# Weighing the values on 64 by 64 array tiles, and taking reciprocals on 16 columns spread by DMA

## The chip, the cores and the metric

The kernel runs on one core of one Trainium2 chip, with TensorE (PE) for matrix products, VectorE (DVE) and ScalarE (ACT) for elementwise work, GpSimd (POOL), and SyncE (SP), which here issues most DMAs. The time is the device time of one execution in microseconds. The kernel before took 3954.87 us, the median of three runs (3951.79 to 3955.97).

## The reference

The input is x, 16 images of 256 channels by 32 x 32 = 1024 positions, in float32. Two layers follow each other. In the first, positions attend to each other with 4 heads of 64 channels; in the second there is a group norm, attention with 8 heads of 32 channels, another group norm and a two-layer perceptron of width 1024. Cut to what matters:

```python
# layer 0
qkv = (xs @ w_proj + b_proj).reshape(B, S, 4, 3 * 64)
attn = softmax(einsum('bihd,bjhd->bijh', q, k) * 64 ** -0.5, axis=2)
res = einsum('bijh,bjhd->bihd', attn, v).reshape(B, S, 256)
x = res @ w_out + b_out + xs
# layer 1
x = x + attention(group_norm(x, 32 groups), 8 heads of 32) @ proj_w.T + proj_b
h = gelu(mlp_w1 @ group_norm(x) + mlp_b1)
x = x + mlp_w2 @ h + mlp_b2
```

## The kernel before

Everything is float32, and one image after another is worked on with its channels on the 128 partitions, in CC = 2 chunks. The 1024 positions are NT = 2 blocks of TB = 512 queries and SB = 8 blocks of 128 keys. Both attentions are written by one function, `attention`; "a" in a name is the first layer, "b" the second.

**The attention.** An item is a pair (t, c) of a query block and a channel chunk, so there are 4 items an image. A unit is an item and a key block, so there are 32 units. For each unit `scores` (L267) makes transposed scores, keys on the partitions, with the array in tiles of 64 x 64 (a; 2 heads a unit) or 32 x 64 (b; 4 heads a unit), and ScalarE takes their exponential e (L279). No maximum is subtracted. `weigh` (L288) then multiplies by the values, with all 128 keys as rows and the head's channels as columns: tiles of 128 x 64 in a, 128 x 32 in b, added up over 8 key blocks in one PSUM bank. VectorE adds the exponentials of the 8 key blocks (es, L305). For the softmax's denominators, `normalise` (L317) multiplies es by a matrix of ones, which puts the sum of each query on all the channels of its head (den); ScalarE copies den to d (L326) and takes exp(-d/DEN_MIN) for a check of range (L329); VectorE takes the reciprocal of 128 x 512 values (L332) and multiplies the weighted values res by it (L333). `project` is the output projection (o in a, j in b, L234), with the sum onto x and the statistics of the group norm on VectorE (L364, L368).

**The order.** Python code writes out the program's order by hand. Attention goes in steps: 3 units of a, or 1 of b; a step writes the scores of its units and then the weighings of the step before, so in a the order is 3 scores, 3 weighings, 3 scores. After each step a `Later` list ticks: `later.after(k, f)` calls f at the k-th tick from then. The denominators of an item come 2 ticks after its last weighing, the projection of a query block 3 ticks after its last denominators. So the projection o(0) comes at step 11 of the 12 of an image, and o(1) after 4 of the 8 hidden pieces that follow. Between the steps of b stand pieces of other work: the perceptron's second product of the image before (m<-g,w), and the first layer's q, k and v of the next image (qk_a, v_a). Between a and b stand the perceptron's first products of the image before (`hidden`, 8 pieces of 8 instructions each, m<-gn_h,w, L536), and q, k, v of the second layer (qk_b, v_b), which need the group norm of a's result (gm_g, gv_g for its means, gn_g for its output). When the program is built, a scheduler still moves instructions of an engine ahead of others where it expects these to wait, so the order in the trace is near that of the code, not the same.

**Projections in strips.** `product` (L234) writes a product in column strips as wide as the list `cols` says: 64 within a, 32 within b, 128 elsewhere.

**PSUM.** Eight banks: three `wide` tiles of two banks, taken in any free slot, for scores, projections and products; and two tiles of one bank (`bank`) for the accumulators, den, and the group norm's small products.

A float32 product is two instructions in the profile, so the 4096 instructions of s_a are 16 x 32 x 4 products.

## Time and profile before

| what | us |
|---|---|
| median of three runs | 3954.87 |
| profiled execution, its own time | 3953.01 |
| span of the profile | 3950.6 |
| TensorE busy | 3923.9 (99%) |
| VectorE busy | 2461.4 (62%) |
| of this RECIPROCAL, d_a and d_b | 214.5 and 214.2 |
| ScalarE busy | 2147.3 (54%) |
| den_a on TensorE | 66.6 |
| SP's DMA queue, share of 16 engines | 2.4% |

A group's line gives the line of code, the engine, the operation, output<-inputs by the program's names, the array tile as rows*columns for a matrix product, the shapes, the count, then busy time and the mean in ns of one, and after the second bar the idle time ahead of it and what ended it. L234 is a helper, so names tell its uses apart. In a timeline a line is a start and a length in us, and the number of equal instructions in a row that it merges; the ends of matrix products are modelled and overlap with the next, so the time that a row of them costs is read from start to start. Tiles that lie beside each other on the array run at once: four of 64 x 64, two of 128 x 64, four of 128 x 32.

### The profile page before, as it was taken

Reading aid. Unit: us, or ns where it says so; the run is one execution under the profiler, and the core shown is the slowest. Engines: PE = TensorE matmul, PEld = TensorE weight load, DVE = VectorE, ACT = ScalarE, POOL = GpSimd, SP = SyncE. Lnnn points to the kernel's source line nnn. Section 1 sums busy time; section 2 is a strip of 40 time slices with the busy share of each in tenths; the row PEclk is TensorE's granted clock in tenths of the full one; section 3 lists DMA queues with packets and bytes.
Section 4 is the critical chain, followed back from the end, with each engine's and each line's share of the span. In section 5 each row is a group of like instructions: output and inputs, shape, how many; then the busy total and the mean of one; then the engine's idle time right before and its main releaser. Section 6 shows DMA issues by size and latency. Waiting matters only on the chain.

```text
span 3950.6 us, 77671 instructions
## 1 busy us (share of the span) xinstructions
PE 3923.9 (99%) x34685; PEld 1407.5 (36%) x34685; DVE 2461.4 (62%) x2539; ACT 2147.3 (54%) x2815; POOL 35.3 (1%) x58
## 2 busy tenths in 40 slices
PE   9999999999999999999999999999999999999998
PEld 3324333343333423334233342333424333343335
DVE  4684756847567475674756747567474665747672
ACT  4654645546455464554645546465564655646461
POOL 1000000000000000000000000000000000000000
PEclk9999999999999999999999999999999999999999
DMA  2000000000000000000000000000000000000000
GB/s 75 1 1 7 17 1 23 1 9 15 1 23 1 9 15 1 23 1 12 12 1 23 1 23 1 1 23 1 23 1 4 20 1 23 1 4 10 1 4 20
DMA packets 18501, 42.80 MB, mean 11 GB/s; under 512 B 3728, under 2 KB 5264, under 8 KB 18160
## 3 DMA queue, kind: packets, MB, share of 16 engines
q1 hardware_dynamic: 13824, 33.56, 2.4%
q8 instruction: 273, 4.47, 0.5%
q10 hardware_dynamic: 3712, 3.80, 0.3%
q0 software_dynamic: 624, 0.41, 0.1%
q14 instruction: 68, 0.56, 0.0%
HBM read 20.99 MB, written 16.78 MB: 10 GB/s over the span
## 4 chain that ended last, share of the span: by engine, by line
PE 98%; issue 1%; DVE 1%; DMA 0%; ACT 0%; POOL 0%; POOLq 0%; DVEq 0%
PE s_b L267 14%; PE acc_b L288 12%; PE s_a L267 12%; PE acc_a L288 12%; PE m L536 12%; PE m L234 11%; PE qk_b L234 6%; PE qk_a L234 5%; PE o L234 3%; PE v_a L234 3%; PE v_b L234 3%; PE j L234 3%; PE den_b L317 1%; PE den_a L317 1%; DVE es_b L305 0%
## 5 line engine op out<-in xcount | busy, mean ns | idle before, releaser
L279 ACT ACTIVATE e_b<-s_b 128x1024 f32<-128x1024 f32 x1024 | 994.2, 1025 | 615.7 <-PE s_b L267 608.7
L305 DVE TENSOR_TENSOR es_b<-es_b,e_b 128x1024 f32<-128x1024 f32 x768 | 895.0, 1221 | 296.6 <-ACT e_b L279 296.6
L267 PE MATMUL s_b<-q,k 32*64 32x512 f32 x8192 | 598.3, 613 | 5.0 <-DVE x L364 3.2
L279 ACT ACTIVATE e_a<-s_a 128x1024 f32<-128x1024 f32 x512 | 487.3, 1026 | 180.1 <-PE s_a L267 180.1
L288 PE MATMUL acc_b<-e_b,v 128*32 128x512 f32 x4096 | 546.0, 604 | 0.0
L305 DVE TENSOR_TENSOR es_a<-es_a,e_a 128x1024 f32<-128x1024 f32 x384 | 466.4, 1215 | 32.2 <-ACT e_a L279 5.5
L267 PE MATMUL s_a<-q,k 64*64 64x512 f32 x4096 | 479.8, 598 | 0.0
L288 PE MATMUL acc_a<-e_a,v 128*64 128x512 f32 x2048 | 477.4, 600 | 0.0
L536 PE MATMUL m<-gn_h,w 128*128 128x512 f32 x1024 | 474.8, 605 | 2.0 <-DVE gn_h L414 2.0
L234 PE MATMUL m<-g,w 128*32 128x256 f32 (+1 forms) x7616 | 464.7, 379 | 0.0
L234 PEld LDWEIGHTS m<-g,w 128*32 128x32 f32 (+1 forms) x7616 | 276.1, 112 | 219.1 <-issue 57.8
L544 ACT ACTIVATE g<-m,m1b 128x512 f32<-128x512 f32 x256 | 170.3, 686 | 317.8 <-PE m L536 317.4
L305 DVE TENSOR_TENSOR es_b<-e_b,e_b 128x1024 f32<-128x1024 f32 x128 | 151.1, 1222 | 234.1 <-ACT e_b L279 234.1
L536 PEld LDWEIGHTS m<-gn_h,w 128*128 128x128 f32 x1024 | 186.1, 190 | 256.4 <-issue 190.7
L267 PEld LDWEIGHTS s_b<-q,k 32*64 32x64 f32 x8192 | 144.8, 129 | 361.9 <-issue 178.8
L332 DVE RECIPROCAL d_a<-d_a 128x512 f32<-128x512 f32 x64 | 214.5, 3352 | 64.4 <-ACT d_a L326 64.4
L234 PE MATMUL qk_a<-x,wp 128*32 128x512 f32 (+1 forms) x1856 | 245.2, 594 | 8.8 <-DMA wp<-in_L_conv_w_proj_dram 6.7
L288 PEld LDWEIGHTS acc_a<-e_a,v 128*64 128x64 f32 x2048 | 132.7, 136 | 331.1 <-issue 331.1
L267 PEld LDWEIGHTS s_a<-q,k 64*64 64x64 f32 x4096 | 139.1, 132 | 304.1 <-issue 264.1
L234 PE MATMUL qk_b<-gn_g,wq 128*32 128x512 f32 (+1 forms) x1280 | 236.9, 593 | 0.0
L288 PEld LDWEIGHTS acc_b<-e_b,v 128*32 128x32 f32 x4096 | 82.2, 108 | 406.7 <-issue 402.5
L458 DVE TENSOR_TENSOR v<-v_b,eones 128x512 f32<-128x512 f32 x64 | 44.3, 692 | 276.2 <-PE v_b L234 276.2
(107 smaller groups left out, 2408.8 us busy)
## 6 DMA issues: line engine op xcount, KB each, us to landing
x<-in_x_dram SPq DMA_DIRECT2D x32, 512.0 KB, 4.5
out_dram<-x SPq DMA_DIRECT2D x64, 256.0 KB, 2.0
w<-in_L_conv_mlp_w_dram ACTq DMA_DIRECT2D x2, 1024.0 KB, 14.9
wq<-in_L_conv_qkv_w_dram ACTq DMA_DIRECT2D x1, 768.0 KB, 11.8
wp<-in_L_conv_w_proj_dram ACTq DMA_DIRECT2D x3, 128.0 KB, 9.7
wp<-in_L_conv_w_proj_dram POOLq DMA_DIRECT2D x3, 128.0 KB, 6.9
wo<-in_L_conv_w_out_dram ACTq DMA_DIRECT2D x1, 256.0 KB, 9.3
wpj<-in_L_conv_proj_w_dram ACTq DMA_DIRECT2D x1, 256.0 KB, 13.5
```

The costliest lines, as they stand in the source:

```text
L234: nc.tensor.matmul(o[sl], w[:, sl], r, **flags)
L267: nc.tensor.matmul(tiles[g // 2][h : h + HALF, g % 2, :], kT[g * D : (g + 1) * D, c, kb * P + h : kb * P + h + HALF], qT[g * D : (g + 1) * ...
L279: nc.scalar.activation(e, s, AF.Exp, scale=scale)
L288: nc.tensor.matmul(accs[i][g * D : (g + 1) * D, :], v_of(c * G + g, kb), es[g // 2][:, g % 2, :], start=(kb == 0), stop=(kb == SB - 1),)
L305: nc.vector.tensor_add(d, held[i][n] if kb == 1 else d, e)
L317: nc.tensor.matmul(den[g * D : (g + 1) * D, :], ones_of(c * G + g), sums[i][g // 2][:, g % 2, :], start=True, stop=True,)
L332: nc.vector.reciprocal(d, d)
L458: nc.vector.tensor_mul(d, ps, v_scale.unsqueeze(1).to_broadcast([P, 2, C // D, D]))
L536: nc.tensor.matmul(ps[:, n, :], k["w1"][:, cc, hc * P : (hc + 1) * P], hn[0][:, cc, t * TB : (t + 1) * TB], start=(cc == 0), stop=(cc == C ...
L544: nc.scalar.activation(g, ps[:, n, :], AF.Gelu, bias=k["m1b"][:, hc : hc + 1])
```

## The change

The function `attention` becomes two.

- In `attention_a` the weighing goes on 64 x 64 tiles as well: the 128 keys of a block are two halves, each with its own accumulator, and the two are added when the item ends (a ScalarE copy and a VectorE addition). An item with an even number has its two accumulators in the `bank` tiles; one with an odd number in wide slot 2, which is kept out of the round meanwhile. A step is now one unit, and a unit's weighing follows its scores by two steps (34 steps an image).
- The denominators of both items of a query block of a are made together, in one bank, each sum on 32 columns in place of 64, so half of the columns pass through the array.
- `denominators` no longer takes the reciprocal of all 128 x 512 values. One row of each 32 is spread by a DMA to 128 x 16 values, VectorE takes their reciprocals, a DMA writes them to DRAM, and 2 (a) or 4 (b) DMAs read them back repeated for the channels. All are issued on SP. The exponential for the range check (`low`) reads d and comes some steps later.
- The wide PSUM tiles have three fixed slots that go round in order.
- o(0) comes at step 25 of 34, in strips of 32 columns; the last j of b comes at step 18 of the next image's a. The means of the second group norm are made on 64 x 64 tiles when they come within a. o(1) is written after 7 of the 8 hidden pieces.
- The result of b is kept in one buffer for each query block, and the second norm's output takes the buffer of q in b.

```diff
-        tc.tile_pool(name="ps_s", bufs=3, space=bass.MemoryType.PSUM)
+        tc.tile_pool(name="ps_s", bufs=1, space=bass.MemoryType.PSUM)
...
+    def wide(name, n=None):
+        while n is None:
+            if turn[0] not in kept:
+                n = turn[0]
+            turn[0] = (turn[0] + 1) % 3
+        return ps_s.tile([P, 2, TB], F32, tag=f"s{n}", name=name)
...
+    def denominators(key, d, n, waits, then, copy):
+        w = 4 * TB // P
...
+        copy(at)
+        nc.sync.dma_start(spread, d[::32].rearrange("p (a b) -> p a b", b=w))
+        def invert():
+            nc.vector.reciprocal(spread, spread)
+            nc.sync.dma_start(row.rearrange("r (a b) -> (r a) b", b=w), spread)
+            num = P * n // (4 * TB)
+            for r in range(P // num):
+                nc.sync.dma_start(
+                    full[r * num : (r + 1) * num], row[r].partition_broadcast(num)
+                )
+            later.after(waits[1], lambda: then(full))
+        def low():
+            nc.scalar.activation(
+                d, d, AF.Exp, scale=-1.0 / DEN_MIN, accum_out=lsum[:, at : at + 1]
+            )
+        later.after(waits[0], invert)
+        later.after(waits[2], low)
...
+        def weigh(i, kb, e):
+            t, c = items[i]
+            if kb == 0:
+                if i % 2:
+                    kept.add(2)
+                    acc = wide(f"acc_{key}_{i}", 2)
+                    accs[i] = [acc[:, h, :] for h in range(2)]
+                else:
+                    accs[i] = [bank(f"acc_{key}_{i}_{h}") for h in range(2)]
+            for h in range(2):
+                for g in range(2):
+                    nc.tensor.matmul(
+                        accs[i][h][g * D : (g + 1) * D, :],
+                        v[h * HALF : (h + 1) * HALF, kb, c * 2 + g],
+                        e[h * HALF : (h + 1) * HALF, g, :],
+                        start=(kb == 0),
+                        stop=(kb == SB - 1),
+                    )
...
+            if kb == SB - 1:
+                r = res[:, c, t * TB : (t + 1) * TB]
+                one, two = accs.pop(i)
+                nc.scalar.copy(r, one)
+                nc.vector.tensor_add(r, r, two)
+                kept.discard(2)
+                if c == CC - 1:
+                    later.after(1, lambda: normalise(t))
+        def normalise(t):
+            half = TB // 2
+            den = wide(f"den_{key}_{t}")[:, 0, :]
+            for c in range(CC):
+                for g in range(2):
+                    for h in range(2):
+                        j = (2 * g + h) * 32
+                        nc.tensor.matmul(
+                            den[j : j + 32, c * half : (c + 1) * half],
+                            k["ones"][:, :32],
+                            sums[t * CC + c][:, g, h * half : (h + 1) * half],
+                            start=True,
+                            stop=True,
+                        )
...
+            denominators(
+                f"{key}_{t}", d, CC * TB,
+                (2, 4, 6) if t < NT - 1 else (1, 1, 26),
...
+            nc.vector.tensor_mul(halves[0], *halves)
+            later.after(1 if t < NT - 1 else 5, lambda: project(t, res))
+        cols[0] = 32
...
+            pending.append(scores(*u))
+            if n >= lag:
+                weigh(*pending.pop(0))
...
# attention_b
-            nc.scalar.activation(
-                den, den, AF.Exp, scale=-1.0 / DEN_MIN, accum_out=lsum[:, at : at + 1]
-            )
-            nc.vector.reciprocal(d, d)
-            nc.vector.tensor_mul(r, r, d)
-            if c == CC - 1:
-                later.after(3, lambda: project(t, res[0]))
+            denominators(
+                f"{key}_{i}", d, TB,
+                ((3, 5, 7) if b + 1 < B else (1, 1, 5)) if last else (1, 3, 4),
...
+            nc.vector.tensor_mul(r, r, full)
+            if c == CC - 1:
+                wait = (10 if b + 1 < B else 1) if last else 1
+                later.after(wait, lambda: project(t, res[t]))
...
# group_norm
+            for n, sl in enumerate(halves):
+                nc.tensor.matmul(
+                    ps[sl, n, :CC], k["gavg"][sl, sl], src[sl], start=True, stop=True
+                )
...
-                    f"h{b}", xs[b], st, k["g2w"], k["g2b"], "gn", hn, 2
+                    f"h{b}", xs[b], st, k["g2w"], k["g2b"], "q1", hn,
+                    4 if b + 1 < B else 2,
```

## The prediction

> **What bounds the kernel.** I read the page's busy totals, the chain that ended last, the costliest groups, and then the timeline of TensorE through one image.

> ```profile
> PE 3923.9 (99%) x34685; PEld 1407.5 (36%) x34685; DVE 2461.4 (62%) x2539; ACT 2147.3 (54%) x2815; POOL 35.3 (1%) x58
> ...
> PE 98%; issue 1%; DVE 1%; DMA 0%; ACT 0%; POOL 0%; POOLq 0%; DVEq 0%
> ...
> L267 PE MATMUL s_a<-q,k 64*64 64x512 f32 x4096 | 479.8, 598 | 0.0
> L288 PE MATMUL acc_a<-e_a,v 128*64 128x512 f32 x2048 | 477.4, 600 | 0.0
> L332 DVE RECIPROCAL d_a<-d_a 128x512 f32<-128x512 f32 x64 | 214.5, 3352 | 64.4 <-ACT d_a L326 64.4
> ```

> TensorE carries 98% of the chain and hardly idles. So VectorE's 428 us of reciprocals (214.5, and 214.2 for d_b) lie beside it; the question is what TensorE's own order costs. Its timeline:

> ```profile
> 2909.52 1.06 PE L288 MATMUL acc_b<-e_b,v 128*32 128x512 f32 x8
> 2910.40 1.91 PE L234 MATMUL v_a<-wp,x 128*32 128x256 f32 x32
> 2912.13 1.04 PE L288 MATMUL acc_b<-e_b,v 128*32 128x512 f32 x8
> 2913.10 2.81 PE L267 MATMUL s_a<-q,k 64*64 64x512 f32 x24
> ...
> 2936.65 2.81 PE L267 MATMUL s_a<-q,k 64*64 64x512 f32 x24
> 2939.39 2.79 PE L288 MATMUL acc_a<-e_a,v 128*64 128x512 f32 x12
> 2942.01 1.03 PE L317 MATMUL den_a<-es_a,ones 128*64 128x512 f32 x4
> 2942.97 2.81 PE L267 MATMUL s_a<-q,k 64*64 64x512 f32 x24
> ```

> Columns: start, length, and the tile's shape before the operands. From start to start, 24 score instructions of 64x64, four abreast, are 6 passes of 512 columns and take 2.74 us; j's 8 passes at 2896-2900 took 3.43, so a pass is 0.429 and 6 are 2.58. The remaining 0.16 stands where the shape changes: acc_b takes 0.88 ahead of v_a of its own shape, 0.97 ahead of s_a. **One change of shape is 0.16 us.** Also important is the end of an image's hidden stage:

> ```profile
> 2999.68 1.02 PE L234 MATMUL o<-res_a,wo 128*128 128x512 f32 x2
> ...
> 3003.62 0.17 DVE L379 COPY mean_c_g<-mv_g 128x2 f32<-128x2 f32 x1
> ...
> 3005.02 0.28 PE L234 MATMUL gm_g<-mean_c_g,gavg 128*128 128x2 f32 x2
> ...
> 3008.23 1.92 DVE L414 TENSOR_SCALAR gn_g<-x,ga_g,gc_g 128x512 f32<-128x512 f32 x4
> ...
> 3013.58 1.02 PE L234 MATMUL qk_b<-gn_g,wq 128*128 128x512 f32 x2
> ```

> o ends at 3000.54. The first two gn tiles, which qk_b needs, are there at about 3009.25: a chain of 8.7 us, wholly under m matmuls.

> [...]

> **The change, part by part**, for one image.

> *Weighing on 64x64.* From 2912.13 to 2984.80 the first attention with its insertions takes 72.67, less 1.71 for four m's in it: 70.96. By counts: 128 passes of attention, and 2 acc_b, 2 den_b, 8 j, 8 o, 8 den_a are 156 x 0.429 = 66.9; 25 changes of shape x 0.16 = 4.0. The sum fits. After: 128 x 64 weighings become twice as many 64 x 64 ones, four abreast, the same passes. Changes of shape: into 64x64, out and back for j with den(0), out and back for o(0), to den(1), to m: 7. So 18 x 0.16 = **2.9 us less**. gm_h and gv_h now fit the shape.

> *Denominators on 32 columns.* den_a falls from 8 passes to 4: 4 x 0.429 = **1.7 us less**. With 0.2 kept back for new seams inside 64x64 (den after acc shows under 0.05), 4.4 x 16 = **70 us**.

> *Reciprocals.* 3352 ns for 512 columns is 6.5 ns each; 16 columns are about 0.17 us. VectorE loses 428 us and gains 96 x 0.17 = 16, 64 additions of a PSUM half at 0.75 (as the 128x512 x line) = 48, and nothing else of size. Worth nothing while TensorE is full. In the last image it isn't: s_b waits 0.85 and 1.82 us there for x's evacuation behind VectorE's queue, and j and gm wait. I take **5 us less**, between 0 and 8.

> *DMAs, all on SP.* Each of 96 denominators issues a spread, a row write and 2 or 4 broadcasts. None of this form is in the trace. Its 256 KB stores land in 2.0 us, its 512 KB loads in 4.5; [...] I take 2.5, so three legs are 7.5 us. Behind a waiting broadcast stand output stores and the next x load, needed an image later: no cost. On VectorE the reciprocal comes one step (3.8 us with a fill) after den in the second attention: den 0.86, copy 0.85 and a leg are 4.2, so it stands 0.4 us, at 4.5 a leg 2.4; behind it stand es additions, and for those the exps, through 8 e buffers. Before, the reciprocal itself held the queue 3.35. Cost 0 to 45 us in all; I take 4.

> *Fixed PSUM slots.* An odd item of the first attention keeps slot 2. Slots go round by a counter that all wide tiles of the program move on; counting it through 16 images, in 11 of 32 odd items (both of images 0 and 1, the second of 3, 5, ... 15) the scores just written lie in slot 2, and the first weighing waits for their exp: 1.03 + 0.2 latency. Elsewhere slot 2 was left a step of 1.72 us earlier. 11 x 1.23 = 14 us, or 0 if the next scores are drawn ahead; I take 8.

> *Last normalisation.* o(1) is written after hidden piece 7 of 8, before after piece 4; gm follows piece 8, and gv and gn stand ahead of qk_b with nothing written between. From gm's start to two gn tiles the trace has 3009.25 - 3005.02 = 4.2 us. Uncovered, 15 x 4.2 = 63 us. But the order on TensorE isn't the written one: o started 8 m's early here, and a last transposition of the program runs at 3884.6, 192 m's ahead of its place. So I expect o to go earlier, or m2 matmuls, which are ready, to fill the hole: 0 to 79 us, taken as 8.

> *Moved, at no cost.* o(0) goes from step 11 of 12 to step 25 of 34, and j from step 4 to step 18, where den(0) shares its excursion; both cost their 8 passes wherever they stand. Their evacuations and statistics (2 x 0.75 + 2 x 0.68 us on VectorE) come ahead of gm_h four steps, 6.9 us, later. In those VectorE has 2.9 + 4 additions of 1.22 + 0.17, about 8 us: hidden only because it also works through j and den (4.3 us); without that cover gm_h would hold TensorE some 1 us an image, 15 us. Each low exp (0.6 us, and 0.2 for its sum) moves some steps on; ScalarE has 1.03 us of exps in each step of 1.72. The output of b's second half in a buffer of its own frees ScalarE's copy from j (74 us of idle time, on an engine busy 54%): nothing. GpSimd keeps its 32 powers; none of its queue is passed.

> Sum: the profiled execution took 3953.0, with span 3950.6. 3953.0 - 70 - 5 + 4 + 8 + 8 = 3898. The median of the runs is 1.9 above the profiled one: **3900 us**.

> **The rivals.**
> (1) Normalisation partly bare, 3 us an image: 37 more, about 3937. For it: as written only piece 8 covers it. Against: the reordering.
> (2) Slower: it is quite bare, as if gm came after o as late as now (8.7 us less piece 8, 3.4): 5.3 x 15 = 79 in place of 8, 3971. The place is one, TensorE ahead of the first qk_b; from 4.2 us an image the gain is gone, from 4.7 the kernel is slower. For it: that now 1.2 us pass between mean_c (3003.79) and gm's place in the order. Against it: m2's input is complete by then.
> (3) The change doesn't do what it says: scores and weighings in one shape still pay the seam. Then 2.9 x 16 = 46 us of the 70 fall away: 3946, at the edge of no change. Against it: acc_b to v_a.
> (4) VectorE standing for late DMAs takes over from the reciprocals in the second attention: 0.8 us of TensorE for each of 64 items, some 50 more: 3950. For it: two exps of 1.03 fill ScalarE to TensorE's own pace there; against it, the idle time of VectorE (es_b waits 531 us for exps).

> **How the numbers follow.** Chances: forecast 0.52, (1) 0.22, (2) 0.12, (3) 0.06, (4) 0.08. A measurement can tell 0.2%, 8 us. Faster: forecast, (1), and a part of (3): 0.79. Same: the rest of (3), most of (4): 0.08. Slower: (2) and a little: 0.13. The forecast's own range, with bounds of the small terms, is 3878 to 3920; the range reaches over (1), (3), (4) to 3962 and leaves out (2) and the best ends.

> **What would show it.** acc_a as 64x64, x4096; some 290 fewer changes of shape; s_a and acc_a alternating at 0.86 us each; den_a at 33 us; RECIPROCAL near 0.17 us x96. Wrong would be: TensorE idle ahead of qk_b by DVE gn_g, above 1 us an image; acc_a above 0.9 us a group; es_b additions waiting behind a reciprocal.

## The result, and the profile after

The kernel after takes 4040.03 us (median, 4038.31 to 4044.91) against 3954.64 us before (here the median of four runs): a ratio of 1.0219, 95% interval 1.0201 to 1.0237. The forecast was 3900 us, faster than before. The profiled execution has a span of 4038.9 us.

The page of the kernel after: busy totals, the shares of the chain that ended last, and one of the groups (busy, mean in ns, after the second bar the idle time ahead).

```profile
PE 3928.3 (97%) x37485; PEld 1461.4 (36%) x37485; DVE 2120.1 (52%) x2569; ACT 2143.3 (53%) x2687; POOL 35.3 (1%) x58
...
PE 93%; DVE 3%; ACT 2%; DMA 1%; issue 1%; POOL 0%; SPq 0%; POOLq 0%; DVEq 0%; ACTq 0%
...
L244 PE MATMUL qk_b<-gn_g,wq 128*32 128x512 f32 (+1 forms) x1280 | 261.6, 617 | 35.2 <-DVE gn_g L576 35.2
```

TensorE's share of the chain fell from 98% to 93%: it now waits. The idle time ahead of qk_b, 35.2 us, had no counterpart before. VectorE's busy time fell by 341 us, and the time did not follow.

First the part that went as forecast. The timeline of TensorE in the first attention of the kernel after (start, length):

```profile
3255.09 1.04 PE L324 MATMUL acc_a<-e_a,v 64*64 64x512 f32 x8
3255.95 1.04 PE L302 MATMUL s_a<-q,k 64*64 64x512 f32 x8
3256.81 1.04 PE L324 MATMUL acc_a<-e_a,v 64*64 64x512 f32 x8
3257.78 3.64 PE L244 MATMUL j<-res_b,wpj 128*32 128x512 f32 x32
3261.24 1.05 PE L354 MATMUL den_a<-es_a,ones 128*32 128x256 f32 x16
```

From start to start, scores and weighings follow each other at 0.86 us for two passes (8 instructions, four at once): 0.43 a pass, and nothing where they alternate. j and den share one excursion. Counted over the trace, TensorE has 64 passes of 512 columns fewer and changes its tiling 1162 times in place of 1428.

Now the end of the hidden stage, on all engines (SPq is the issue of a DMA). It is the stretch that the prediction showed of before, one chain from the spread of den(1) to qk_b:

```profile
3048.05 0.59 SPq L262 DMA_DIRECT2D sp_a<-d_a  x1
...
3049.93 0.25 DVE L265 RECIPROCAL sp_a<-sp_a 128x16 f32<-128x16 f32 x1 [4.21 <-DMA sp_a<-d_a]
3050.22 0.34 SPq L266 DMA_DIRECT2D row_a<-sp_a  x1
...
3051.73 1.10 SPq L269 DMA_DIRECT2D rd_a<-row_a  x2
...
3056.34 1.23 DVE L377 TENSOR_TENSOR res_a<-res_a,rd_a 128x1024 f32<-128x1024 f32 x1 [6.16 <-DMA rd_a<-row_a]
...
3067.15 1.12 PE L244 MATMUL o<-res_a,wo 128*128 128x512 f32 x2
...
3078.60 0.28 PE L244 MATMUL gm_g<-mean_c_g,gavg 128*128 128x2 f32 x2
...
3079.72 0.38 PE L244 MATMUL gv_g<-tv_g,gavg 128*128 128x2 f32 x2 [0.84 <-DVE tv_g L556]
...
3081.76 1.92 DVE L576 TENSOR_SCALAR gn_g<-x,ga_g,gc_g 128x512 f32<-128x512 f32 x4
...
3082.45 9.80 PE L244 MATMUL qk_b<-gn_g,wq 128*128 128x512 f32 x16 [2.35 <-DVE gn_g L576]
```

The multiplication by rd_a is done at 3057.57, yet o starts at 3067.15: not a late DMA but o's place in TensorE's order holds it. After o stand only 16 m instructions, and all of them come ahead of gm_g. So gv_g and qk_b wait bare (0.84 and 2.35 us), and the last of the m's has itself waited 0.78 us for ScalarE. And qk_b then takes 9.64 us from start to start (v_b starts at 3092.09) where 16 such instructions are 16 x 0.429 = 6.87. The windows of the kernel after show why (columns: the window, its length, busy time and instructions of PE, PEld, DVE, ACT and POOL, the granted clock, the DMA's share, GB/s):

```profile
3067.00:3082.00 15.00, 11.48 (x29) 5.07 (x28) 4.55 (x16) 4.00 (x7) 0.69 (x1) 0.97 0.00 0
3082.00:3092.00 10.00, 9.55 (x16) 4.18 (x17) 1.67 (x4) 1.75 (x3) 0.00 (x0) 0.71 0.00 0
```

Here TensorE stood 3.5 of the 15 us before, and the clock falls to 0.71 over the next ten. This is image 12 (counted from 0), one of the worst. The same three waits come in 15 images, but qk_b then takes 6.94 us in two of them, 8.64 in nine and 9.5 to 9.7 in four: the granted clock is at 0.50 for 3.41 us in the nine and for 6.83 in the four, and stays at 1.00 in the two. For comparison, the place in the kernel before, and then image 2 of the kernel after, where the clock stayed full in spite of the waits:

```profile
3014.00:3024.00 10.00, 10.00 (x28) 5.00 (x27) 0.00 (x0) 4.35 (x7) 0.00 (x0) 1.00 0.00 0
...
580.42:590.42 10.00, 9.55 (x29) 5.45 (x30) 2.35 (x5) 3.62 (x5) 0.00 (x0) 1.00 0.00 0
```

A second place is in the first attention, in images with an odd number. The timeline of all engines of the kernel after:

```profile
3271.87 1.23 DVE L377 TENSOR_TENSOR res_a<-res_a,rd_a 128x1024 f32<-128x1024 f32 x1 [2.68 <-DMA rd_a<-row_a]
...
3274.15 0.32 DVE L550 COPY mean_h<-gm_h 64x2 f32<-64x2 f32 x2
...
3275.11 0.22 PE L533 MATMUL gv_h<-tv_h,gavg 64*64 64x2 f32 x2 [2.25 <-DVE tv_h L556]
...
3276.45 2.11 PE L324 MATMUL acc_a<-e_a,v 64*64 64x512 f32 x8
```

VectorE stands 2.68 us for rd_a. Behind it in its queue stand gm_h's small copies, whose product ended at 3269.4; gv_h waits for them on TensorE, and the weighing after it takes 2.05 us from start to start in place of 0.86: the half clock again (granted 0.50 from 3276.45 to 3278.56; by the clock's record in five of the eight odd images).

To see where the time is, the starts of the instructions give each image three stretches: a, from the first s_a to the end of its last acc_a; h+q, from there to the first s_b (hidden pieces, o(1), norm, q, k, v); and b, from there to the next s_a, with the tail in the last image. Sums over 16 images in us:

| kernel | a | h+q | b |
|---|---|---|---|
| before | 1096.6 | 752.1 | 2063.2 |
| after | 1073.3 | 851.8 | 2076.9 |

One den_b (0.99 us an image) moved from a to b; without that, b is the same. h+q lost 99.7 us: 6.6 us an image in 15 images. In a 68.77 us became 65.2 in even images and 67.8 to 69.8 in odd ones, where 63.2 was to be expected (68.77 - 2.9 - 1.7 - 0.99).

### The profile page after: what moved, and what is told of

The parts are those of the page before. It is cut to its first block, busy times and chain, and to the rows that moved or that the text cites. A ratio compares the mean times of both kernels' runs of the same rounds, so it can differ in the third digit from the quotient of the medians.

```text
span 4038.9 us, 84302 instructions
## 1 busy us (share of the span) xinstructions
PE 3928.3 (97%) x37485; PEld 1461.4 (36%) x37485; DVE 2120.1 (52%) x2569; ACT 2143.3 (53%) x2687; POOL 35.3 (1%) x58
## 4 chain that ended last, share of the span: by engine, by line
PE 93%; DVE 3%; ACT 2%; DMA 1%; issue 1%; POOL 0%; SPq 0%; POOLq 0%; DVEq 0%; ACTq 0%
PE s_b L411 13%; PE acc_b L432 12%; PE m L244 11%; PE m L692 11%; PE acc_a L324 10%; PE s_a L302 10%; PE qk_b L244 6%; PE qk_a L244 6%; PE o L244 3%; PE v_a L244 3%; PE v_b L244 3%; PE j L244 3%; PE den_b L464 2%; DVE es_a L336 1%; ACT g L700 1%
## 5 line engine op out<-in xcount | busy, mean ns | idle before, releaser
L310 ACT ACTIVATE e_a<-s_a 128x1024 f32<-128x1024 f32 x512 | 520.3, 1023 | 404.6 <-PE s_a L302 394.1
L302 PE MATMUL s_a<-q,k 64*64 64x512 f32 x4096 | 591.1, 596 | 0.2 <-DVE res_a L341 0.2
L324 PE MATMUL acc_a<-e_a,v 64*64 64x512 f32 x4096 | 588.0, 595 | 3.2 <-ACT e_a L310 3.2
L244 PEld LDWEIGHTS m<-g,w 128*32 128x32 f32 (+1 forms) x7616 | 277.9, 112 | 217.7 <-issue 65.2
L244 PE MATMUL qk_b<-gn_g,wq 128*32 128x512 f32 (+1 forms) x1280 | 261.6, 617 | 35.2 <-DVE gn_g L576 35.2
L324 PEld LDWEIGHTS acc_a<-e_a,v 64*64 64x64 f32 x4096 | 183.1, 134 | 292.2 <-issue 226.2
L302 PEld LDWEIGHTS s_a<-q,k 64*64 64x64 f32 x4096 | 172.5, 133 | 275.5 <-issue 211.5
L514 DVE SCALAR_TENSOR_TENSOR x<-o,bvo,x 128x512 f32<-128x512 f32 x64 | 45.1, 747 | 285.5 <-PE o L244 284.6
L244 PEld LDWEIGHTS qk_b<-gn_g,wq 128*32 128x32 f32 (+1 forms) x1280 | 88.5, 133 | 186.3 <-issue 161.4
```

The costliest lines, as they stand in the source:

```text
L244: nc.tensor.matmul(o[sl], w[:, sl], r, **flags)
L302: nc.tensor.matmul(s[h : h + HALF, g, :], kT[g * D : (g + 1) * D, c, kb * P + h : kb * P + h + HALF], qT[g * D : (g + 1) * D, c, t * TB : ...
L310: nc.scalar.activation(e, s, AF.Exp, scale=float(D) ** -0.5)
L324: nc.tensor.matmul(accs[i][h][g * D : (g + 1) * D, :], v[h * HALF : (h + 1) * HALF, kb, c * 2 + g], e[h * HALF : (h + 1) * HALF, g, :], st ...
```

## The experiments

Theories, by the letters of the expectations: **N**, the norm's chain is bare and the clock falls after it; **D**, the DMAs are late and TensorE waits for them; **S**, the fixed wide slots; **V**, VectorE's queue stands for rd_a and holds gm_h's copies. T, W and R are named where they come. Each run changes the kernel after, unless another is named. In brief, with ratios to the kernel before:

| run | time, us | ratio | a | h+q |
|---|---|---|---|---|
| e17_before_o_late (of before) | 4052.82 | 1.0251 [1.0235, 1.0267] | 1096.6 | 850.1 |
| e1_o_early | 3979.69 | 1.0070 [1.0053, 1.0087] | 1073.9 | 787.1 |
| e2_keep_busy | 4024.74 | 1.0179 [1.0162, 1.0196] | 1077.3 | 830.5 |
| e13_o_mid | 3951.29 | 0.9999 [0.9991, 1.0008] | 1071.9 | 763.1 |
| e3_scale_later | 4045.58 | 1.0231 [1.0214, 1.0248] | 1074.9 | 855.7 |
| e4_both | 4009.66 | 1.0144 [1.0127, 1.0161] | 1082.5 | 806.1 |
| e5_low_early | 4045.90 | 1.0237 [1.0220, 1.0254] | 1076.1 | 850.1 |
| e6_gmh_early | 4046.46 | 1.0231 [1.0214, 1.0248] | 1077.1 | 850.6 |
| e7_three | 3984.28 | 1.0076 [1.0059, 1.0093] | 1071.0 | 792.2 |
| e8_three_slot | 3986.09 | 1.0088 [1.0071, 1.0105] | 1059.9 | 805.8 |
| e10_den_bank | 4037.66 | 1.0212 [1.0195, 1.0229] | 1123.1 | 794.2 |
| e11_gmh_late | 4007.11 | 1.0139 [1.0122, 1.0156] | 1065.6 | 818.2 |
| e12_weigh128 | 4071.60 | 1.0302 [1.0285, 1.0319] | 1157.4 | 793.1 |
| e14_gmh_late_alone | 4010.18 | 1.0145 [1.0130, 1.0161] | 1048.1 | 844.3 |
| e15_mid_and_late | 3925.08 | 0.9928 [0.9915, 0.9942] | 1048.4 | 761.2 |
| e16_gm_banks | 3949.85 | 0.9991 [0.9983, 1.0000] | 1065.3 | 767.2 |
| e18_gmh_ten | 3925.74 | 0.9931 [0.9918, 0.9945] | 1036.1 | 773.0 |

### The place of o(1)

**In the kernel before, o(1) alone is moved.**

```diff
-                later.after(3, lambda: project(t, res[0]))
+                later.after(6 if D == D0 and t == NT - 1 else 3, lambda: project(t, res[0]))
```

> The kernel before with one edit: o(1) comes 3 hidden pieces later, after 7 of the 8, as in the kernel after. If o(1)'s place alone bares the norm's chain and halves the clock after it: the hidden stage and q, k, v together grow from 752 us to 830-855, the time from 3954 to 4030-4050, as much as the mending of it took from the kernel after (89). If the stall needs the change's other parts (fixed slots, spread DMAs): under 3990.

It takes 4052.82 us, 99.5 more than before and 3 above the expected range. The stretch h+q grows by 98.0, and the first attention stays at 68.77 us an image to the hundredth. Its TensorE timeline shows the waits of the kernel after:

```profile
3087.12 0.35 PE L234 MATMUL gv_g<-tv_g,gavg 128*128 128x2 f32 x2 [0.93 <-DVE tv_g L393]
3089.73 8.81 PE L234 MATMUL qk_b<-gn_g,wq 128*128 128x512 f32 x16 [2.25 <-DVE gn_g L414]
```

Here there are no spread DMAs, no fixed slots and no one-shape attention. o(1)'s place does it by itself, and theories D and S fall for this stretch.

**The same place, mended in the kernel after**: first as early as it goes, then between.

```diff
-            later.after(1 if t < NT - 1 else 5, lambda: project(t, res))
+            later.after(1, lambda: project(t, res))                        # e1_o_early
+            later.after(1 if t < NT - 1 else 3, lambda: project(t, res))   # e13_o_mid
```

> The changed kernel with o(1) written one hidden piece after its scaling in place of five, so that gm, gv and gn have hidden pieces written after them. Theory N (the slowing is the norm's chain standing bare ahead of qk_b, and the half clock that follows): the hidden stage and q, k, v of an image lose about 6.6 us in 15 images, so about 100 us: 3930 to 3950, level with or a little faster than the kernel before. Theory D (the repeated reciprocals come late from DRAM, so that o can't go sooner): o waits for rd_a instead, less than 30 us gained, 4010 or more. Theory S (the three fixed PSUM slots hold the hidden pieces up): m still waits for g, 60 us or less gained.

> The kernel after, with o(1) 3 ticks after its multiplication in place of 5 (1 in the first experiment), so that it comes after 5 of the 8 hidden pieces, in two halves between m pieces, as before the change. If o(1)'s place is what made the hidden stage long, and its earliest place is what made m wait for slots: the hidden stage and q, k, v together fall from 851.7 us to 752-765, the granted clock stays full, and the time is 3945 to 3960, at the time of before. If den's wide slot or the low exponential is to blame: as in the first experiment, 3975 to 3985.

e1 gains 60 us, not the 90 and more that theory N expected: the chain is covered and the clock nearly full (0.997 on the mean of the profiled execution, 0.990 in the kernel after), but in its stead m now waits for ScalarE (24.5 us in all). TensorE and ScalarE in the timeline of e1:

```profile
3011.39 1.28 ACT L276 ACT_TABLE_LOAD   x1
...
3013.42 1.28 ACT L700 ACT_TABLE_LOAD   x1
...
3015.45 3.70 PE L692 MATMUL m<-gn_h,w 128*128 128x512 f32 x8 [1.96 <-ACT g L700]
```

e13 puts o in halves between m's, after 32 m instructions of the 64, so that gm_g comes with m's behind it. It gains 88.7 us, lies at the time of the kernel before, and its h+q is 763.1, inside the expected 752 to 765. So the earliest place was too early and the changed one too late.

**How much of it is the clock**: products whose results aren't used keep TensorE busy behind gm and gv.

```diff
+            keep_busy(f"w1_{key}", 1, st["mean_c"])   # one 128x512 product after gm
+            keep_busy(f"w2_{key}", 3, st["tv"])       # three after gv
```

> The changed kernel with one idle product of 128x512 after gm and three after gv, whose results are not used, in the two holes ahead of qk_b; the chain itself stays bare. Theory N with the half clock as a part of its own: the granted clock stays at 1 through qk_b and 1.7 to 2.7 us an image come back, so 25 to 35 us less than the changed kernel: 4005 to 4015. If the clock is no part (qk_b is slow for another reason, as its weights), no change or up to 10 us slower: 4040 to 4050.

TensorE in the timeline of e2:

```profile
3075.77 7.03 PE L244 MATMUL qk_b<-gn_g,wq 128*128 128x512 f32 x16
3082.64 7.07 PE L244 MATMUL v_b<-wq,gn_g 128*128 128x256 f32 x32
```

qk_b is back at 6.87 us, and the mean granted clock of the profiled execution at 0.996. The part from qk_b to s_b falls from a mean of 15.7 to 13.87 us in every image, 27 us in all. The hidden part grows by 6 and the first attention by 4, so that the kernel gains 15, less than the 25 to 35 expected. Of the 99.7 us that h+q lost in the kernel after, then, 27 are the clock and some 73 are not: in the list of waits, 48 stand ahead of gv_g and qk_b, and 20 ahead of m, which waits for ScalarE's g. In e17, whose qk_b takes 8.65 to 9.85 us, the same reading gives 35 of the 98 to the clock.

### VectorE's queue

Three edits try to get gm_h's copies and the multiplication apart: the multiplication 2 ticks later (e3), gm_h 2 ticks earlier (e6), gm_h 4 ticks later (e14).

```diff
-                (2, 4, 6) if t < NT - 1 else (1, 1, 26),
+                (2, 6, 8) if t < NT - 1 else (1, 1, 26),   # e3_scale_later
...
-                    4 if b + 1 < B else 2,
+                    2,                                      # e6_gmh_early
+                    8 if b + 1 < B else 2,                  # e14_gmh_late_alone
```

> The changed kernel with the scaling of the first query block of the first attention two steps later (and its range check too), so that VectorE doesn't stand for rd_a ahead of the small copies of gm_h. Theory V ([...] in odd images gm_h's copies stand behind the scaling that waits for its DMA, and TensorE for gv_h): the odd images' 67.8 to 69.8 us of first attention come to about 65.5, 8 x 3.5 = 28 us less: about 4012. Theory S (the odd images' slots are to blame): they keep their excess, within 8 us of the changed kernel.

> The kernel after, with gm_h called 2 ticks after its statistics in every image in place of 4, so that its small copies come on VectorE ahead of the multiplication that waits for rd_a. Theory V (in odd images VectorE stands for rd_a, gm_h's copies stand behind it, gv_h waits on TensorE and the clock halves): the odd images' first attention falls from 67.8-69.8 to about 66, some 20 to 30 us, 4010 to 4020. Theory S (the fixed slots make odd images long): no change there, 4040.

> The kernel after, with gm_h 8 ticks after its statistics in place of 4 and nothing else. The first attention becomes alike in both parities at 65.2 to 66.8 us (67.1 on the mean in the kernel after): 5 to 25 us less than 4040, 4015 to 4035. The hidden stage keeps its 38.2 us and its half clock.

e3 and e6 miss. In e3 the scheduler still puts the multiplication ahead of the copies on VectorE, and gv_h now waits in 14 images. In e6 gm_h's copies do come first and gv_h waits no more, but the next step of the same norm (rstd_h) then stands behind the multiplication, and scores that take gv_h's slot wait for it: 18.2 us in 8 waits, the longest 3.1.

e14, with both steps behind the multiplication, makes the two parities alike: 65.4 us in nearly every image, 25 us less in a, and 29.9 us in the whole. The waits of e14 still have "VectorE for rd_a" at 148.4 us, more than the 123.0 of the kernel after. So it isn't VectorE's standing that cost, but what stood behind it: with only additions of es there, the eight e buffers cover it, and TensorE's list of waits in e14 has none of that size that follows from it. That is theory V, and R falls.

e3 together with e1 (theory: the two gains add) is e4:

> The two edits together, o(1) early and the scaling of the first block later. If theories N and V are two separate causes their gains add: about 4040 - 100 - 28 = 3912, 1% faster than the kernel before. If one only moves the other's wait, 3940 or more.

They don't add: 30 us worse than e1 alone, 8.6 of it in a and 19.0 in h+q. In h+q m waits 33.2 us against 26.3 in e1, and the clock is at half there for 27.3 us against 3.4 (on the mean of the whole execution it is 0.990 against 0.997), worth up to 12 us (an estimate: half of the difference). Together that is about the 19.

### Other suspects

**The range check's exponential** (L276), taken from den right after the copy as in the kernel before (e5), and with e1 and e6 together (e7):

```diff
+        nc.scalar.activation(den, den, AF.Exp, scale=-1.0 / DEN_MIN, accum_out=lsum[:, at : at + 1])
...
-        later.after(waits[2], low)
```

> The kernel after, but the exponential of the range check is taken from den in PSUM straight after ScalarE's copy to d, as before the change, so that none falls between the gelus of the hidden stage. Theory T (the exponential among the gelus, with its two table loads, makes the m pieces wait for a PSUM tile, and puts o still later): m's waits for ACT g ahead of qk_b go, 0.8 to 1.8 us an image, 10 to 25 us in all: 4015 to 4030 from 4040. Theory N (the bare norm chain alone, 2.6 us and 1.1 us and the half clock after it): that chain is untouched and the time stays within 8 us of 4040.

> The kernel after with three edits together: o(1) one tick after its multiplication (the first experiment), the range check's exponential straight after the copy, gm_h after 2 ticks. If the three waits are the whole of what the forecast missed: 3980 less 20 to 30 in the hidden stage less 16 to 30 in the odd images, 3915 to 3940, faster than before by 0.4 to 1 per cent. If they hide one another (one chain, of which the longest link counts), about 3960 to 3980.

e5 gains nothing (4045.9, within 8 us of the kernel after, as theory N has it). Theory T falls for the kernel after. e7 lies at e1's time, a little above its second outcome: where o is as early as it goes, m waits for ScalarE with or without it.

**The slots.** In e8 an odd item's accumulator takes the slot used longest ago:

```diff
-                    kept.add(2)
-                    acc = wide(f"acc_{key}_{i}", 2)
+                    keep[0] = turn[0]
+                    kept.add(keep[0])
+                    acc = wide(f"acc_{key}_{i}", keep[0])
```

> The same three edits, and the odd item's accumulator takes the wide slot that comes round next, the one used longest ago, in place of slot 2. Theory S as the prediction has it (11 of 32 odd items wait for the exponential of the scores just written): about 8 us less than with the three edits, 3907 to 3932; if the scheduler draws other scores ahead meanwhile, the same time as with three.

The first attention gets 11.1 us shorter than in e7, 2.7 of it in image 0 with its two clashing items; h+q gets 13.6 longer, as the hidden part, 33.1 us in even and 34.8 in odd images of e7, is now 34.8 in all. In the kernel after, and in e7, 11 weighings wait for an exponential just written, in the very items that the prediction counted; in e8 none does. At the 2.7 us of image 0's two, 11 would cost some 15 us (an estimate), near the 14 that the prediction worked out and above the 8 that it took. Mending it was given back in another stage.

**den(1) in an accumulator's bank** (e10, on top of e1 and e5), and gm_h late as well (e11). Theory W: den and o(1) hold two of three wide slots.

```diff
-            den = wide(f"den_{key}_{t}")[:, 0, :]
+            den = wide(name)[:, 0, :] if t < NT - 1 else bank(name)
```

> The kernel after with o(1) one tick after its multiplication, the range check's exponential straight after the copy, and the denominators of the second query block of a in a bank of the accumulators (free by then) in place of one of the three wide slots. Theory W (in the hidden stage den and o(1) hold two of the three wide slots, so that m waits for ScalarE in the third; before, den lay in a bank): the hidden stage falls from 33.2-34.0 us to the 31.7 of before, 20 to 35 us of the whole against 3980 with o(1) early alone: 3945 to 3960. If the table loads of the exponential are to blame, or the order, the stage stays at 33 to 34.8 and the time at 3975 to 3985.

> The kernel before this one in the list, with gm_h 8 ticks after its statistics in place of 4, so that gm_h's and gv_h's copies come on VectorE behind the multiplication that waits for rd_a, and TensorE behind o(0). Theory V (what makes the first attention 67 to 70 us in odd images is TensorE waiting, in a fixed slot, for gm_h's or gv_h's copies while VectorE stands for rd_a): both parities come to about 65, some 2 us an image on the mean, 25 to 40 us less than without: 3910 to 3930, faster than before the change. Rival R (VectorE's standing for rd_a also holds the additions of es, and through them the buffers of e, whoever else is queued): no more than 10 us less.

W falls: the hidden part stays at 34.0 us. And e10's first attention is longer than in any other run but e12, since V now strikes in every image but the first: gv_h waits on TensorE for its copies 15 times, 42.1 us in all, where the kernel after has 19.2 us in 8. With gm_h late this is gone and a is 66.80 us in both parities, but the hidden part is 35.7 us: m waits 43.7 us for ScalarE in place of 30.8, and den(1) 10.6 us for VectorE's last additions, which is nearly all that h+q grew by. e11 is 30.6 us faster than e10, as V has it (25 to 40), though far from the time expected of it.

**The price of a change of shape.** e12 is e11 with the values weighed on 128 x 64 again, still one unit a step.

```diff
-            for h in range(2):
-                for g in range(2):
-                    nc.tensor.matmul(accs[i][h][g * D : (g + 1) * D, :], v[h * HALF : (h + 1) * HALF, kb, c * 2 + g], ...)
+            for g in range(2):
+                nc.tensor.matmul(accs[i][g * D : (g + 1) * D, :], v[:, kb, c * 2 + g], e[:, g, :], ...)
```

> The same with gm_h late, but the values weighed on tiles of 128 x 64 again, one accumulator in a bank, still one unit a step: s_a and acc_a alternate in two shapes, 64 changes in 32 units where all in one shape has none. Theory of the prediction (a change of shape is 0.16 us): 57 more an image, 9 us, 146 us in all, about 4060 to 4080. If the gain of one shape were not real (the rival in which one shape pays the seam too): the same time as the kernel with gm_h late, within 20 us.

TensorE in the timeline of e12:

```profile
2511.17 1.08 PE L315 MATMUL acc_a<-e_a,v 128*64 128x512 f32 x4
2512.18 1.09 PE L299 MATMUL s_a<-q,k 64*64 64x512 f32 x8
2513.20 1.08 PE L315 MATMUL acc_a<-e_a,v 128*64 128x512 f32 x4
```

Two passes take 1.015 us here and 0.858 in one shape: 0.157 for each change, as forecast, and the rival of one shape paying the seam falls. The trace has 55 changes more an image than e11's (57 were expected): 8.7 us. The first attention grew by 5.7, to 72.5, which is what e12's own passes and changes come to (146.5 x 0.429 + 62 x 0.157 = 72.6). e11's 66.8 lie 3 us above its own count (146.5 x 0.429 + 7 x 0.157 = 63.9), in waits that e12, whose accumulators need no wide slot, doesn't have. h+q fell by 25 in the whole, 23 of it in the waits of den(1) and m, so that 64.5 us of the 146 are seen in the time. That 4071.60 lies in the expected range is luck: the range was counted from a time of e11 that e11 missed by 77 us.

### Both places mended

e15 is e13 and e14 together. e16 then takes gm_h's and gv_h's products out of the wide slots into the accumulators' banks; e18 is e15 with gm_h at 10 ticks.

```diff
-            later.after(1 if t < NT - 1 else 5, lambda: project(t, res))
+            later.after(1 if t < NT - 1 else 3, lambda: project(t, res))
...
-                    4 if b + 1 < B else 2,
+                    8 if b + 1 < B else 2,    # 10 in e18_gmh_ten
...
-                    ps[sl, n, :CC], k["gavg"][sl, sl], src[sl], start=True, stop=True
+                    ps[n][sl, :CC], k["gavg"][sl, sl], src[sl], start=True, stop=True    # e16: two banks
```

> Both edits: o(1) 3 ticks after its multiplication and gm_h 8 ticks after its statistics. If these two places are what the forecast missed, the gains add: the first attention at 65.2 to 66.8 us, the hidden stage at 31.7 to 32.5 us: 3920 to 3945, faster than before by 0.2 to 0.8 per cent. If they don't add (as the first and third experiments together), 3960 to 4000.

The gains nearly add: 88.7 and 29.9 alone, 115.0 together. At 3925.08 us it is 0.72% faster than the kernel before, and beats both edits alone. TensorE in the timeline of e15, at the end of the hidden stage:

```profile
2505.60 0.28 PE L244 MATMUL gm_g<-mean_c_g,gavg 128*128 128x2 f32 x2
...
2506.81 0.35 PE L244 MATMUL gv_g<-tv_g,gavg 128*128 128x2 f32 x2
...
2510.62 1.12 PE L244 MATMUL qk_b<-gn_g,wq 128*128 128x512 f32 x2
```

Between gm_g and gv_g stand 2 m instructions, between gv_g and qk_b 8, and no wait is left there. In its first attention one larger wait remains, on all engines of e15:

```profile
2462.78 1.41 DVE L514 SCALAR_TENSOR_TENSOR x<-o,bvo,x 128x512 f32<-128x512 f32 x2
...
2467.02 0.32 DVE L550 COPY mean_h<-gm_h 64x2 f32<-64x2 f32 x2
...
2467.39 1.09 PE L302 MATMUL s_a<-q,k 64*64 64x512 f32 x8 [0.96 <-DVE mean_h L550]
```

gm_h's product ran at 2464.4. Its copies now stand behind o(0)'s sums and statistics, and scores wait for gm_h's slot. The two runs that go after it:

> The kernel with o(1) 3 ticks after its multiplication and gm_h 8 ticks after its statistics, and within a the small products of gm_h and gv_h lie in the two banks of the accumulators, free by then, in place of a wide slot. If the fixed slots are what is left of the first attention (65.4 us where passes and changes of shape come to 63.3): it falls to 63.5-64, 1.2 to 2 us an image, 18 to 30 us in all, 3895 to 3908, the forecast's own number. If the wait lies in VectorE's copies whatever holds them: 3920 to 3927.

> The kernel with o(1) 3 ticks and gm_h 8 ticks after, but gm_h 10 ticks after its statistics. If the scores' wait behind gm_h is VectorE's queue after o(0): that wait goes, 1.0 to 1.7 us an image, the first attention falls from 65.4 to 63.7-64.4 us and the time from 3925 to 3900-3910, the forecast's number. If it comes from the slot whatever VectorE does, 3920 to 3928; if gn_h now comes late for the first m, the hidden stage grows by as much.

Neither gains. e16 is 24.8 us slower than e15, outside both of its outcomes: gm_h waits for an accumulator to leave its bank (0.76 us), its second half for the copy of the first (0.62), and den(1) for VectorE's last additions (0.49), in 15 images each. In e18 the wait is gone, and the first attention falls by 0.8 us an image; but gn_h's 1.92 us now push the last additions on VectorE back, and den(1) waits for them, 12.9 us in 15 waits. h+q grows by 0.8 us an image: the third outcome of its expectation. The wait changes its place and, in e18, keeps its size.

## Why the prediction was wrong

**The step that failed is "Last normalisation".** It had the chain's length about right, 4.2 us from gm to two gn tiles (3.85 measured from gm to qk_b, which set out after the first tile), and the place, and it priced the bare chain at 63 and bounded it at 79. But it took 8, on the ground that the scheduler would move o further ahead or fill the hole with m2. It did neither. It drew o ahead by 8 m instructions, the same number as in the kernel before (24 m's ahead of o where 32 were written; now 48 where 56 were), and m2 stayed behind qk_b; why the scheduler left it there isn't shown. That o had moved once was read as proof that it would move as needed. With the 8 m's accounted for, the count was to be had from the written order: 64 - 48 leaves 16 m's, four groups, of which o's own halves and its sums and statistics on VectorE (3.1 us from o's end to mean_c, as before) take all. Measured: 98 us by o(1)'s place alone in the kernel before.

**What was missing altogether** is the clock, 35 of these 98, and 27 of the 99.7 in the kernel after. Waits of 0.78, 0.84 and 2.35 us within 6.5 us were enough in 13 of 15 images; qk_b took up to 2.8 us more.

The same three waits cost different amounts: qk_b takes 6.94 us in two images, 1.7 to 2.8 us more in the others. In image 13 of the kernel after, TensorE is busy for 31% of the time from 3333.65 to 3337.06, still at a granted clock of 1.00, and the 3.41 us after are at 0.50. In image 2 it is busy for 58% of the time from 575.70 to 579.11 and for 49% of that from 579.11 to 582.53, and the clock stays at 1.00. A stall on TensorE was priced at its length, where on the average it came to about 1.4 times that here (99.7 for 73).

**"Moved, at no cost" failed in part**: gm_h beside the spread DMA cost 30 us. The step named gm_h's four steps and VectorE's load in them, some 15 us without cover, but it added up busy times only. What held the copies was a wait: VectorE stood 2.68 us for rd_a, and mean_h's copies ran at 3274.15, behind the multiplication that it stood for (3271.87) and one addition of es. The prediction counted on such standing for the es additions of the second attention (rival 4), not for the small copies that TensorE waits for.

**What held.** A change of shape: 0.157 us against 0.16 (single ones differ: the prediction's own acc_b lines have 0.09 from acc_b to s_a). den_a: 4 passes fewer an image. In the image of e15 shown, a and b together are 1.8 us shorter than before, and three waits in its first attention come to 2.1 (1.20 at 2467.39, and 0.42 and 0.46 ahead of o and behind gv_h, by the same reading from start to start): 3.9, against 4.4 forecast. The gain of the change is there once it isn't waited away. The DMA legs of den(1) took 1.9, 1.5 and 4.6 us, 8.0 against 7.5. The last image's second attention and tail fell from 182.7 to 179.4, 3.3 against 5. b cost nothing, so rival 4 fell; rival 3 fell with e12. The reciprocal of 16 columns took 0.25 us, not 0.17: per column isn't all of it.

**Of the rivals** (2) was the right one, "as if gm came after o as late as now", at 79 us in place of 8. It gave 3971; the clock's 27 us and gm_h's 30 are most of what it lacked to 4040. The fixed slots, taken as 8, held in their direct cost (11 clashes in the items counted), but they also decide where other waits go, and e8, e16 and e18 moved such waits without making the whole shorter.

**Image 0's first attention**, with no other image's work in it, needs 65.12 us, as before (65.04), where 60 were to be expected. Its passes and changes come to 60.5 in the trace (138.5 x 0.429 + 7 x 0.157), and 1.0 at its start was there before too. The two items' slots are 2.7 (e8: 62.40), and 1.0 is a wait of scores, after the first odd item, for the slot that its accumulators leave.

## What to carry to other kernels

When a step is moved later in front of a dependent chain, count what is still left in the order to cover the chain after the move, instruction by instruction, and take the scheduler to move things only as far as it did before. Price a stall on TensorE with the slower clock that may follow (99.7 us for 73 of waits here), and look for what stands behind a waiting instruction in its queue rather than at how long it waits: 148 us of VectorE's waiting cost little once the small copies that TensorE needs stood elsewhere. Freeing an engine that isn't the bound (341 us of VectorE here) is worth what its queue lets through, which may be nothing.
